# A decoder layer's ternary weights: transposes on TensorE or by DMA, and VectorE's order by the scheduler or as written

## The chip, the core and the metric

The kernel runs on one core of a Trainium2 chip. Five engines with instruction streams of their own share an SBUF of 128 partitions: PE (TensorE, matrix products and transposes into PSUM), DVE (VectorE), ACT (ScalarE), POOL (GpSimd) and SP (SyncE, which here only issues DMAs). The metric is device time in microseconds (us), lower is better.

## The reference

One layer of a decoder in float32, on x of 4 x 512 rows of 512 numbers, with a context of 4 x 1024 rows. Its three parts, cut to their core:

```python
# 1. local attention (on layernorm(x)), added to x
q = h @ wq_comp @ wq_up                       # 512 -> 128 -> 16 heads of 128
q = rmsnorm(partial_rope(q)); k = rmsnorm(partial_rope(h @ wk)); v = h @ wv
mask = (diff >= 0) & (diff < 128)             # each row sees 128 keys
probs = softmax(concat([where(mask, q k^T / sqrt(128), -1e30), sink]))
x = x + group_matmul(probs[..., :t] @ v, out_w1) @ out_w2
# 2. cross attention to the 1024 context rows, 16 heads of 32, ALiBi, masked
# 3. feed forward with quantised weights and activations
def weight_quant(w):
    scale = 1.0 / clip(mean(abs(w)), EPS)
    return clip(round(w * scale), -1.0, 1.0) / scale
# gate and up: 2048 x 512, down: 512 x 2048; einsum('bsh,oh->bso', act_quant(x), weight_quant(w))
```

The three weights of the third part are thus reduced to -1, 0 and 1 times one number for each. The products contract over the weights' last axis, so the kernel needs each of them transposed.

## The kernel before, in words

The 2048 rows are 16 tiles of 128 (`xres`, kept in SBUF). The kernel has three stages: A, local attention, up to about 690 us; B, cross attention, to about 1430 us; C, the feed forward. The diff touches stage A alone, in which the ternary weights for stage C are made beside the attention.

Stage A's unit is one tile and one group of four heads: 64 units. The main loop (L766) is a software pipeline with one unit entering in each iteration n. In this order, iteration n does: `turn` of unit n (L654: transposes of the roped queries, `qtr`); `weights` of unit n-1 (L683: exponentials on ACT, `den` and its reciprocal on DVE, the scaling of `p` on POOL); `queries` of unit n+1 (L645: the matmul `q_ps`, then `rope`); one step of `before`; `scores` of unit n (L661: `sc`, then mask, maximum and small operations on DVE); `values` of unit n-2 (L708: `av`); one step of `prep`; `turn_weights` of unit n-1 (L699: `ptr`, then `pT` on DVE). Between them `fill` (L726) takes matmuls out of generators that wait for a place:

- `before(b)` (L455) makes what batch b's units need. In each of its first four steps it normalizes a tile into `h` (L122, DVE) and transposes it (`tr_ps`, L130, PE); for batches 1 to 3 the first step also takes the statistics of four tiles (`row_stats`, L83: L88 and L89 on DVE, then `veps`, L97, and a power on POOL, L81). Two steps of `qc_ps`, four of `kv_ps` with their rope, and `ktr` follow. Batch 0 is done ahead of the loop, with statistics tile by tile; batches 1, 2 and 3 begin at iterations 0, 16 and 32, one step in each iteration.
- `fold` (L511) multiplies the two output weights into one, at the start; while it lasts (`many`) no step of `prep` is taken.
- `project` (L541) is the output projection of a finished tile, 16 matmuls `y` and one add to `xres` on DVE (L548).
- `prep` is first `ternary_weights` (L550), and from iteration 61 on `first_rows` (L741), which begins stage B: statistics of batch 0 on DVE (`norm_of`, L101), a power on POOL, `shift` and the normalized rows on ACT (L109 to L117), and their transposes.

`rope` (L435) squares on ACT, and does two products, a sum and a row sum on DVE (L442 to L448) with a power on POOL.

`ternary_weights` first reads all three weights and sums their absolute values, 12 chunks of 1 MB in 12 steps. Then it reads the 12 chunks again. A chunk is `raw`, 512 x 512 numbers in four blocks of 128 rows; six operations of DVE, three on each half (L588 to L590), turn it into the bf16 tile `tern` (one buffer). Each of two groups of eight PE transposes (L598) fills one PSUM bank, `wtr`, that ACT copies to `wst` (L603, two buffers), and SP stores that to DRAM (L606), where stage C loads it from. A chunk takes three steps; the copies are taken in the middle of the next iteration (L788).

What sets the order: inside `tc.manual_schedule(engines={PE, Activation})` (L735) the named engines keep the order in which the program emits their instructions. Instructions of the other engines, DVE among them, are put in order by a planner in the framework, which may move an instruction ahead of others that are written before it, as far as data and buffers allow. Each engine then runs its own list strictly from first to last, and waits at an instruction whose data are not there. DMAs are issued by the engine that the program names, here nearly always SP, in that engine's order.

Of the kernel before, what the change touches and what calls it, by code (L numbers as in the profile page):

```python
# [14 lines left out]
BF16 = mybir.dt.bfloat16  # L15
# [3 lines left out]
ALU = mybir.AluOpType  # L19
# [3 lines left out]
P = 128  # L23
# [17 lines left out]
MAGIC = 12582912.0  # L41
# [9 lines left out]
def decoder_layer(  # L51
# [7 lines left out]
    nc = tc.nc  # L59
# [12 lines left out]
    ident_b = const.tile([P, P], BF16, name="ident_b")  # L72
# [53 lines left out]
    def transpose_rows(pool, src, dst, tag="tr", copy=None):  # L126
# [9 lines left out]
    ternary = {  # L136
        "g": dram.tile([P, DC, FF], BF16, name="tern_g"),
        "u": dram.tile([P, DC, FF], BF16, name="tern_u"),
        "d": dram.tile([P, FC, D], BF16, name="tern_d"),
    }  # L140
# [229 lines left out]
    with tc.tile_pool(name="aw", bufs=1) as aw, tc.tile_pool(name="akv", bufs=2) as akv, \  # L370
# [7 lines left out]
        ap = early.enter_context(tc.tile_pool(name="ap", bufs=2, side="right"))  # L378
# [29 lines left out]
            out=older, in_=older, compare_op=ALU.is_ge, fill=1.0, base=0,  # L408
# [5 lines left out]
            out=older_t, in_=older_t, compare_op=ALU.is_gt, fill=0.0, base=0,  # L414
# [5 lines left out]
            out=newer_t, in_=newer_t, compare_op=ALU.is_gt, fill=1.0, base=0,  # L420
# [129 lines left out]
        def ternary_weights():  # L550

            ones = aw.tile([P, 1], F32, name="ones")
            nc.gpsimd.memset(ones, 1.0)
            invs = aw.tile([P, 3], F32, name="invs")

            def chunk(n, k):
                raw = ap.tile([P, 4, 512], F32, tag="w2", name="raw")
                w = (w_gate, w_up, w_down)[n]
                of = w[:, ts(k, 512)] if n == 2 else w[ts(k, 512)]
                nc.sync.dma_start(out=raw, in_=of.rearrange("(r p) n -> p r n", p=P))  # L560
                return raw

            for n in range(3):
                part = small.tile([P, 8], F32, tag="part", name="part", bufs=1)
                for k in range(4):
                    raw = chunk(n, k)
                    for h in range(2):
                        nc.vector.tensor_reduce(
                            part[:, 2 * k + h:2 * k + h + 1], raw[:, 2 * h:2 * h + 2, :], AX.XY, ALU.add,
                            apply_absolute_value=True,  # L570
                        )
                    yield
                tot_ps = fp.tile([P, 8], F32, tag="f", name="tot_ps")
                nc.tensor.matmul(
                    tot_ps, lhsT=ones.to_broadcast([P, P]), rhs=part, start=True, stop=True
                )
                mean = small.tile([P, 1], F32, tag="mean", name="mean", bufs=1)
                nc.vector.tensor_reduce(mean, tot_ps, AX.X, ALU.add)
                nc.vector.tensor_scalar(mean, mean, 1.0 / (FF * D), Q_EPS, ALU.mult, ALU.max)
                nc.vector.tensor_scalar(steps[:, n:n + 1], mean, 1.0 / 128.0, None, ALU.mult)  # L580
                nc.vector.reciprocal(invs[:, n:n + 1], mean)
            for n, dst in enumerate(ternary.values()):
                for k in range(4):
                    raw = chunk(n, k)
                    tern = ap.tile([P, 4, 512], BF16, name="tern", bufs=1)
                    for h in range(2):
                        r = raw[:, 2 * h:2 * h + 2, :]
                        nc.vector.tensor_scalar(r, r, invs[:, n:n + 1], -1.0, ALU.mult, ALU.max)  # L588
                        nc.vector.tensor_scalar(r, r, 1.0, MAGIC, ALU.min, ALU.add)
                        nc.vector.tensor_scalar(  # L590
                            tern[:, 2 * h:2 * h + 2, :], r, MAGIC, None, ALU.subtract
                        )
                    yield
                    for c0 in (0, 2):
                        ps = fp.tile([P, 2, 512], BF16, tag="f", name="wtr")
                        for c in range(2):
                            for r in range(4):
                                nc.tensor.transpose(  # L598
                                    ps[:, c, ts(r, P)], tern[:, r, ts(c0 + c, P)], ident_b
                                )  # L600
                        yield "copy"
                        st = ap.tile([P, 2, 512], BF16, tag="w1", name="wst")
                        nc.scalar.copy(st, ps)  # L603
                        to = dst[:, 4 * k + c0:4 * k + c0 + 2, :] if n == 2 else \
                            dst[:, c0:c0 + 2, ts(k, 512)]
                        nc.sync.dma_start(out=to, in_=st)  # L606
                        yield

        def mask_rows():

# [121 lines left out]
                        break  # L732
                    del behind[first]

        with tc.manual_schedule(engines={mybir.EngineType.PE, mybir.EngineType.Activation}):  # L735
            for i, _ in enumerate(before(0)):
                if i >= 5:
                    fill(2)
            units = [Unit(n) for n in range(NT * G)]

            def first_rows():  # L741

                rows_two = rows_of(0)
                for i in range(QT + 1):
                    next(rows_two)
                    if i % 2 == 0:
                        yield
                first.turn(0)
                yield
                first.keys(0)  # L750
                yield
                queries(0, 0)
                yield
                first.turn(1)
                yield
                queries(0, 1)
                yield
                first.keys(1)

            for b in range(1, B):  # L760
                nc.sync.dma_start(
                    out=xres[:, b * QT:(b + 1) * QT, :], in_=x[b].rearrange("(t p) d -> p t d", p=P)
                )
            units[0].queries()
            soon, prep, step = iter(()), ternary_weights(), None
            for n in range(len(units) + 2):  # L766
                if n == len(units) - 3:
                    for _ in prep:
                        pass
                    early.close()  # L770
                    bx = late.enter_context(tc.tile_pool(name="bx", bufs=1, side="right"))
                    bank.update(pool=fp, tag="f")
                    first = KeysValues(0)
                    prep = first_rows()
                if n % (QT * G) == 0 and n // (QT * G) + 1 < B:
                    soon = before(n // (QT * G) + 1)
                many = "fold" in behind
                if n < len(units):
                    units[n].turn()
                if 1 <= n <= len(units):  # L780
                    units[n - 1].weights()
                fill(2)
                if n + 1 < len(units):
                    units[n + 1].queries()
                next(soon, None)
                if n < len(units):
                    units[n].scores()
                if step == "copy":  # L788
                    step = next(prep, None)
                fill(2 if many else 1)  # L790
                if not many and n >= len(units) - 1:
                    next(prep, None)
                if n >= 2:
                    units[n - 2].values()
                fill(1 if many else 1 + n % 2)
                if not many:
                    step = next(prep, None)
                fill(1 if many else 0)
                if 1 <= n <= len(units):
                    units[n - 1].turn_weights()  # L800
                fill(1 if many else 0)
                if n == QT * G:
                    cross_weights()
                    masks = mask_rows()
                if QT * G + 10 <= n < QT * G + 15:
                    next(masks)
            for _ in prep:
                pass
            while behind:
                fill(1)  # L810
# [27 lines left out]
    with tc.tile_pool(name="b1", bufs=1) as b1, \  # L838
# [204 lines left out]
        for b in range(1, B):  # L1043
            at = KT * HG * (b - 1)
# [43 lines left out]
        with tc.manual_schedule(engines={mybir.EngineType.PE}):  # L1088
# [18 lines left out]
            for step in range(-2, KT * SETS + KT):  # L1107
                m, kt = divmod(step, KT)
                now = 0 <= step < KT * SETS
                ahead, i0 = divmod(step + 10, KT)  # L1110
# [14 lines left out]
                ps = weights(m, kt, sts) if now else None  # L1125
# [19 lines left out]
    with tc.tile_pool(name="c1", bufs=1) as c1, \  # L1145
# [6 lines left out]
                engines={mybir.EngineType.PE, mybir.EngineType.DVE, mybir.EngineType.Activation}  # L1152
# [205 lines left out]
```

## Time and profile before

| | |
|---|---|
| median of 3 runs | 1727.3 us (1725.91 to 1728.79) |
| the profiled execution | 1726.91 us, its span 1725.2 us |
| mean granted clock of TensorE | 0.987 |
| busy: PE, DVE, ACT, POOL | 1644.0, 1148.4, 946.2, 737.5 us |
| PE busy from 0 to 100 us | 81.85 us |
| PE busy from 100 to 200 us | 98.8 us |
| PE busy in each 100 us from 200 to 600 | 100 us |
| PE busy from 600 to 700 us | 96.88 us |
| `wst<-wtr`, ACT copies of the transposed ternary weights | 24 of 1.017 us, from 283.4 to 594.2 us |
| `tern<-raw`, third DVE operation of a half chunk | 24 of 0.684 us, from 255.5 to 563.7 us |

How to read it: the span is the time from the first to the last instruction of one profiled execution. A row of the timeline gives start, duration, engine, line, operation, output and inputs, shapes, and in brackets how long the engine was idle before it and what ended that. In the rows of windows, each engine has its busy time in the window and its number of instructions, then come the clock granted to TensorE (1 is full speed), the share of DMA time and GB/s. "SPq" and the like are the instruction queues that issue DMAs.

### The profile page before, as it was taken

The numbers are of one execution on the slowest core, as the hardware profiler recorded it, in microseconds if no ns is written. First come the engines' busy times: TensorE is split into PE (matmuls) and PEld (weight loads), VectorE is DVE, ScalarE is ACT, GpSimd is POOL, SyncE is SP. The second block draws the span as 40 slices with busy tenths as digits, with TensorE's granted clock in tenths as the row PEclk, the third lists the DMA queues.
The fourth block names the chain that finished last, engine by engine and source line by source line (L and its number), as shares of the span: only waits on it lengthen the run. The fifth ranks groups of instructions, "written<-read, shape, count | busy, mean of one in ns | idle before, by whom it ended". The sixth has DMA issues, their size and how long they took to land.

```text
span 1725.2 us, 23227 instructions
## 1 busy us (share of the span) xinstructions
PE 1644.0 (95%) x8064; PEld 949.4 (55%) x8096; DVE 1148.4 (67%) x2312; ACT 946.2 (55%) x1834; POOL 737.5 (43%) x470
## 2 busy tenths in 40 slices
PE   7899999999999999799999999999999978999997
PEld 4556556655655555555555555555544425666664
DVE  4555887877777662565656565656567527989996
ACT  1444455566556653145544554454566645888876
POOL 2212222322223220358878787878778970000000
PEclk9999999999999999889999999999999989999999
DMA  8421231121111000421212121211121110000000
GB/s 255 136 98 74 79 117 61 43 74 54 57 44 42 25 1 25 104 56 45 57 26 68 40 56 26 70 38 45 26 75 50 33 56 2 13 13 20 13 20 25
DMA packets 68709, 93.28 MB, mean 54 GB/s; under 512 B 23044, under 2 KB 29832, under 8 KB 68168
## 3 DMA queue, kind: packets, MB, share of 16 engines
q1 hardware_dynamic: 67296, 90.58, 17.2%
q0 software_dynamic: 1152, 1.15, 0.3%
q8 instruction: 64, 1.05, 0.2%
q14 instruction: 53, 0.43, 0.1%
q10 hardware_dynamic: 144, 0.07, 0.0%
HBM read 61.76 MB, written 10.86 MB: 42 GB/s over the span
## 4 chain that ended last, share of the span: by engine, by line
PE 81%; DVE 7%; ACT 5%; issue 3%; SPq 1%; POOL 1%; DMA 1%; ACTq 0%; POOLq 0%; DVEq 0%
PE y L544 13%; PE s_ps L870 8%; PE st L918 6%; PE sc L666 6%; PE o_ps L953 5%; PE xo_ps L1011 3%; PE q_ps L290 3%; PE q_ps L647 3%; PE av L711 3%; PE f_ps L533 3%; PE st L929 3%; PE av L713 2%; PE d_ps L1245 2%; PE y_ps L1211 2%; PE u_ps L1175 2%
## 5 line engine op out<-in xcount | busy, mean ns | idle before, releaser
L942 POOL TENSOR_TENSOR sum<-sum,p 128x1024 f32<-128x1024 f32 x190 | 446.3, 2375 | 37.8 <-ACT p L936 37.6
L874 DVE TENSOR_REDUCE nm<-s_ps 128x1 f32<-128x512 f32 x512 | 319.4, 682 | 165.4 <-PE s_ps L870 165.3
L936 ACT ACTIVATE p<-st 128x1024 f32<-128x1024 f32 x256 | 249.3, 1020 | 86.3 <-PE st L929 82.2
L544 PE MATMUL y<-wf,attnT 128*128 128x512 f32 x512 | 246.8, 592 | 0.0
L695 POOL TENSOR_TENSOR p<-p,den 128x512 f32<-128x512 f32 x64 | 67.7, 1057 | 407.9 <-ACT sq L438 252.5
L870 PE MATMUL s_ps<-ks,qs 99*128 99x512 f32 x512 | 199.9, 460 | 23.2 <-DVE nm L874 12.7
L870 PEld LDWEIGHTS s_ps<-ks,qs 99*128 99x128 f32 x512 | 88.5, 191 | 176.0 <-DVE nm L874 60.2
L918 PE MATMUL st<-qs,ks 101*128 101x512 f32 x512 | 165.9, 405 | 4.7 <-ACT p L936 4.3
L953 PE MATMUL o_ps<-p,va 128*32 128x512 f32 x1024 | 136.6, 606 | 0.0
L544 PEld LDWEIGHTS y<-wf,attnT 128*128 128x128 f32 x512 | 91.9, 190 | 73.6 <-issue 71.7
L688 ACT ACTIVATE p<-s,nm,rs 128x128 f32<-128x128 f32 x256 | 123.2, 485 | 0.9 <-DVE nm L678 0.6
L942 POOL TENSOR_TENSOR sum<-p,p 128x1024 f32<-128x1024 f32 x32 | 75.2, 2372 | 111.8 <-ACT p L936 91.6
L918 PEld LDWEIGHTS st<-qs,ks 101*128 101x128 f32 x512 | 95.6, 191 | 35.9 <-ACT p L936 20.2
L666 PE MATMUL sc<-kT,qT 128*128 128x256 f32 (+1 forms) x512 | 107.6, 353 | 0.0
L81 POOL TENSOR_TENSOR rs<-ss,neghalf 128x4 f32<-128x4 f32 (+1 forms) x72 | 82.6, 1151 | 53.4 <-DVE ss L448 52.3
L659 ACT COPY qT<-qtr 128x512 f32<-128x512 f32 x64 | 37.5, 586 | 121.5 <-PE qtr L657 121.5
L666 PEld LDWEIGHTS sc<-kT,qT 128*128 128x128 f32 x512 | 88.6, 190 | 25.8 <-issue 16.3
L720 ACT COPY attnT<-av 128x512 f32<-128x512 f32 x64 | 37.5, 587 | 86.9 <-PE av L713 70.3
L1175 PEld LDWEIGHTS <-xqT 128*128 128x128 bf16 x512 | 50.1, 98 | 48.0 <-issue 1.5
L1015 DVE TENSOR_TENSOR xres<-xo_ps,xres 128x512 f32<-128x512 f32 x64 | 44.3, 691 | 44.7 <-PE xo_ps L1011 42.4
L1011 PE MATMUL xo_ps<-wo_sb,oT 128*128 128x512 f32 x128 | 65.3, 636 | 7.6 <-POOL oT L1000 4.8
L704 DVE TENSOR_TENSOR pT<-ptr,newer_t 128x512 f32<-128x512 f32 x64 | 43.9, 686 | 40.0 <-PE ptr L702 40.0
(193 smaller groups left out, 3033.6 us busy)
## 6 DMA issues: line engine op xcount, KB each, us to landing
cx<-in_ctx SPq DMA_DIRECT2D x32, 256.0 KB
raw<-in_L_ffn_w_gate SPq DMA_DIRECT2D x8, 1024.0 KB
raw<-in_L_ffn_w_up SPq DMA_DIRECT2D x8, 1024.0 KB
raw<-in_L_ffn_w_down SPq DMA_DIRECT2D x8, 1024.0 KB
qs<-qH SPq DMA_DIRECT2D x128, 64.0 KB
w<-in_L_attn_out_w SPq DMA_DIRECT2D x4, 1024.0 KB
w<-in_L_attn_out_w SPq DMA_DIRECT2D x16, 256.0 KB
qs<-qL SPq DMA_DIRECT2D x64, 64.0 KB
```

Source lines behind the costliest of these rows:

```text
L81: nc.gpsimd.tensor_tensor(dst, src, neghalf[:, :src.shape[1]], ALU.pow)
L544: nc.tensor.matmul(y, lhsT=attnT[:, h, :], rhs=wf[:, h, :], start=(h == 0), stop=(h == HEADS - 1))
L666: nc.tensor.matmul(sc[:, h, first * P:], lhsT=self.qT[:, h, :], rhs=kT[:, (qt - 1 + first) * P:(qt + 1) * P], start=True, stop=True,)
L688: nc.scalar.activation(self.p[:, h, :], s[:, h, :], AF.Exp, bias=nm[:, h:h + 1], scale=self.rs[:, h:h + 1], accum_out=den[:, h:h + 1],)
L870: nc.tensor.matmul(s_ps, lhsT=qss[hh][0:R_TOP, g, ts(qt, P)], rhs=kss[b % 2][0:R_TOP, g, ts(hf, T)], start=True, stop=True,)
L874: nc.vector.tensor_reduce(nms[m][:, qt, g, hf:hf + 1], s_ps, AX.X, ALU.max, negate=True)
L918: nc.tensor.matmul(st[:, g % 2, :], lhsT=ks[0:R_TOP + 2, g, ts(kt, P)], rhs=qss[hh][0:R_TOP + 2, g, :], start=True, stop=False,)
L936: nc.scalar.activation(p, st, AF.Exp)
L942: nc.gpsimd.tensor_tensor(sums[m][i], last[i] if kt == 1 else sums[m][i], ps[i], ALU.add)
L953: nc.tensor.matmul(accs[m][at, :], lhsT=va[:, kt, at], rhs=ps[g // 2][:, g % 2, :], start=(kt == 0), stop=(kt == KT - 1),)
L1011: nc.tensor.matmul(y_ps, lhsT=oTs[m][:, ts(qt, P)], rhs=wo_sb[:, hh, :], start=True, stop=True)
L1175: nc.tensor.matmul(acc, lhsT=xqTs[self.t][:, c, :], rhs=w[c][:, ts(n, 512)], start=(c == 0), stop=(c == DC - 1),)
```

## The change

Three things are changed together.

First, the ternary chunks are transposed by DMA. PE's transposes, the PSUM tile `wtr` and ACT's copies are gone; in their place SP issues eight transposing DMAs for each chunk, each of which reads a 128 x 256 piece of `tern` and writes it transposed into `wst`, in SBUF. The stores to DRAM follow as before.

Second, the six DVE operations of a chunk, all in one step before, are spread over the chunk's three steps, two in each, and a chunk's load of `raw` is issued one chunk ahead, after the first operation of the chunk before it.

Third, DVE is named in the manual schedule of stage A: its instructions keep the order in which the program emits them.

```diff
-            for n, dst in enumerate(ternary.values()):
-                for k in range(4):
-                    raw = chunk(n, k)
-                    tern = ap.tile([P, 4, 512], BF16, name="tern", bufs=1)
-                    for h in range(2):
-                        r = raw[:, 2 * h:2 * h + 2, :]
+            chunks = [(n, k) for n in range(3) for k in range(4)]
+            ahead = chunk(0, 0)
+            for at, (n, k) in enumerate(chunks):
+                raw, dst = ahead, tuple(ternary.values())[n]
+                tern = ap.tile([P, 4, 512], BF16, name="tern", bufs=1)
+                halves = [raw[:, 2 * h:2 * h + 2, :] for h in range(2)]
+                for i in range(6):
+                    r, of = halves[i // 3], tern[:, 2 * (i // 3):2 * (i // 3) + 2, :]
+                    if i % 3 == 0:
                         nc.vector.tensor_scalar(r, r, invs[:, n:n + 1], -1.0, ALU.mult, ALU.max)
+                    elif i % 3 == 1:
                         nc.vector.tensor_scalar(r, r, 1.0, MAGIC, ALU.min, ALU.add)
-                        nc.vector.tensor_scalar(
-                            tern[:, 2 * h:2 * h + 2, :], r, MAGIC, None, ALU.subtract
+                    else:
+                        nc.vector.tensor_scalar(of, r, MAGIC, None, ALU.subtract)
+                    if i == 0 and at + 1 < len(chunks):
+                        ahead = chunk(*chunks[at + 1])
+                    if i % 2:
+                        yield
+                for c0 in (0, 2):
+                    st = ap.tile([P, 2, 512], BF16, tag="w1", name="wst")
+                    for r in range(4):
+                        nc.sync.dma_start_transpose(
+                            out=st[:, :, ts(r, P)], in_=tern[:, r, ts(c0 // 2, 2 * P)]
                         )
-                    yield
-                    for c0 in (0, 2):
-                        ps = fp.tile([P, 2, 512], BF16, tag="f", name="wtr")
-                        for c in range(2):
-                            for r in range(4):
-                                nc.tensor.transpose(
-                                    ps[:, c, ts(r, P)], tern[:, r, ts(c0 + c, P)], ident_b
-                                )
-                        yield "copy"
-                        st = ap.tile([P, 2, 512], BF16, tag="w1", name="wst")
-                        nc.scalar.copy(st, ps)
-                        to = ...
-                        nc.sync.dma_start(out=to, in_=st)
-                        yield
+                    to = ...
+                    nc.sync.dma_start(out=to, in_=st)
...
-        with tc.manual_schedule(engines={mybir.EngineType.PE, mybir.EngineType.Activation}):
+        with tc.manual_schedule(
+            engines={mybir.EngineType.PE, mybir.EngineType.Activation, mybir.EngineType.DVE}
+        ):
...
-                if step == "copy":
-                    step = next(prep, None)
...
-                    step = next(prep, None)
+                    next(prep, None)
```

The order of PE's other instructions, and of ACT's, is the same in both kernels. In the new order of DVE, a step of `before` stands where the loop writes it: in iteration n behind `den` and its reciprocal of unit n-1 and behind the rope of unit n+1, and ahead of mask and maximum of unit n.

More of the change, by code (lines that the diff above doesn't have):

```diff
@@ L588, in ternary_weights @@
                         nc.vector.tensor_scalar(r, r, invs[:, n:n + 1], -1.0, ALU.mult, ALU.max)
+                    elif i % 3 == 1:
                         nc.vector.tensor_scalar(r, r, 1.0, MAGIC, ALU.min, ALU.add)
-                        nc.vector.tensor_scalar(
-                            tern[:, 2 * h:2 * h + 2, :], r, MAGIC, None, ALU.subtract
-                        )
-                    yield
-                    for c0 in (0, 2):
-                        ps = fp.tile([P, 2, 512], BF16, tag="f", name="wtr")
-                        for c in range(2):
-                            for r in range(4):
-                                nc.tensor.transpose(
-                                    ps[:, c, ts(r, P)], tern[:, r, ts(c0 + c, P)], ident_b
-                                )
-                        yield "copy"
-                        st = ap.tile([P, 2, 512], BF16, tag="w1", name="wst")
-                        nc.scalar.copy(st, ps)
-                        to = dst[:, 4 * k + c0:4 * k + c0 + 2, :] if n == 2 else \
-                            dst[:, c0:c0 + 2, ts(k, 512)]
-                        nc.sync.dma_start(out=to, in_=st)
-                        yield
@@ new lines, in ternary_weights @@
+                    else:
[9 more added lines that the diff above has]
+                            out=st[:, :, ts(r, P)], in_=tern[:, r, ts(c0 // 2, 2 * P)]
+                        )
+                    to = dst[:, 4 * k + c0:4 * k + c0 + 2, :] if n == 2 else \
+                        dst[:, c0:c0 + 2, ts(k, 512)]
+                    nc.sync.dma_start(out=to, in_=st)
@@ L764, in decoder_layer @@
             units[0].queries()
-            soon, prep, step = iter(()), ternary_weights(), None
+            soon, prep = iter(()), ternary_weights()
             for n in range(len(units) + 2):
```

## The prediction

> **What bounds the kernel now.** I read the page's first two parts, then the chain of work that ended last, then the windows of the stage that the diff touches, and last the timelines of PE and DVE at the places where the order changes.
>
> ```profile
> PE 1644.0 (95%) x8064; PEld 949.4 (55%) x8096; DVE 1148.4 (67%) x2312; ACT 946.2 (55%) x1834; POOL 737.5 (43%) x470
> ...
> PE   7899999999999999799999999999999978999997
> ...
> PE 81%; DVE 7%; ACT 5%; issue 3%; SPq 1%; POOL 1%; DMA 1%; ACTq 0%; POOLq 0%; DVEq 0%
> ```
>
> TensorE is busy 95% of the span and carries 81% of the last chain. The windows say it for the part with the ternary work (columns: PE, PEld, DVE, ACT, POOL busy with instruction counts, clock, DMA share, GB/s):
>
> ```profile
> 200.00:300.00 100.00, 100.00 (x384) 58.29 (x383) 84.93 (x218) 53.04 (x156) 29.08 (x26) 1.00 0.30 107
> ...
> 500.00:600.00 100.00, 100.00 (x414) 58.22 (x413) 70.63 (x196) 60.66 (x173) 27.09 (x24) 1.00 0.09 32
> ```
>
> Between 200 and 600 us PE never waits, and DVE has 15 to 29% to spare. So PE work taken out there counts in full, ACT or DVE work taken out counts for nothing, and any new wait of PE counts in full too. PE's order is written by hand and is the same in both kernels but for the transposes taken out. What must be asked is whether DVE, until now put in order by the scheduler, still delivers in time. Two stretches of PE's timeline, the second at a group of ternary transposes:
>
> ```profile
> 224.87 1.02 PE L647 MATMUL q_ps<-wqu_sb,qcT 128*128 128x512 f32 x2
> 225.72 0.60 PE L130 MATMUL tr_ps<-ident,h 128*128 128x128 f32 x4
> 226.16 1.06 PE L666 MATMUL sc<-kT,qT 128*128 128x128 f32 x8
> ...
> 389.97 0.61 PE L598 MATMUL wtr<-ident_b,tern 128*128 128x128 bf16 x8
> 390.42 0.60 PE L702 MATMUL ptr<-ident,p 128*128 128x128 f32 x4
> ```
>
> In the first, which is iteration 16, tile 16's layernorm output h is turned straight after the next unit's query matmul, without a wait. DVE in the same microseconds, then BN and the power of 4 variances elsewhere:
>
> ```profile
> 226.03 0.16 DVE L693 TENSOR_TENSOR den<-den,es 128x4 f32<-128x4 f32 x1 [1.83 <-ACT es L692]
> 226.23 0.18 DVE L694 RECIPROCAL den<-den 128x4 f32<-128x4 f32 x1
> 226.37 0.55 DVE L122 TENSOR_SCALAR h<-xres,mv,rstd 128x512 f32<-128x512 f32 x1
> 226.83 0.42 DVE L442 TENSOR_TENSOR ra<-q_ps,cos_sb 128x256 f32<-128x256 f32 x1
> ...
> 228.15 0.42 DVE L445 TENSOR_TENSOR q<-ra,rb 128x256 f32<-128x256 f32 x1
> 228.48 0.17 DVE L448 TENSOR_SCALAR ss<-ss 128x4 f32<-128x4 f32 x1
> ...
> 599.66 0.69 DVE L88 BATCH_NORM_STATS2 stats<-xres 128x6 f32<-128x512 f32 x1
> 600.39 0.18 DVE L89 BATCH_NORM_AGGREGATE mv<-stats 128x2 f32<-128x6 f32 x1
> ...
> 35.11 1.01 POOL L81 TENSOR_TENSOR rstd<-veps,neghalf 128x4 f32<-128x4 f32 x1 [3.20 <-DVE veps L97]
> ```
>
> The h at 226.37 is that of tile 17, whose transposes come a whole iteration later: the scheduler had moved normalizations, and the statistics before them, ahead of where the program writes them. The written order has h behind the rope operations (L442 to L448).
>
> **The change part by part.** First, what goes. 24 groups of eight bf16 transposes leave PE, each 390.42 − 389.97 = 0.45 us of issue: −10.8 us, all on the path, since PE is at 100% there. 24 ACT copies of 1.017 us go too (24.4 us); ACT is busy 53 to 61%, so nothing is counted. The six ternary operations per chunk stay, spread over three slots where one slot held all; they stand before waits DVE already has (1.83 us before den in the fence), so 0. The cover is that slack; without it the two operations, 0.68 us each, would cost 1.4 us in each of 36 slots, 49 us.
>
> Second, the DMA transposes: 96 of 128x256 bf16, 64 KB each, on SP's queue, eight in a chunk, then two stores. DVE's first write to the single tern buffer of the next chunk waits for all eight. A chunk lasts three slots, 26 us (slots are 8.6 to 10.3), and from a chunk's last DVE operation to the next chunk's first write about two slots, 16 us, pass. With 7 us of DVE steps and waits between the halves, they are hidden while (26 − 7)/8 ≈ 2.4 us each holds. No transposing DMA is in this trace. Bounds from the nearest rows: from below 0.32 to 0.38 us, the issue of a ternary store by SP; from above 3.3 us, issue to landing of the 64 KB copy from SBUF to SBUF (ks from kH). The nearest in kind are 64 KB loads in 128-byte runs (wq_sb, L164): 0.65 to 1.6 us each. At 1.6 a chunk takes 8 × 1.6 + 7 ≈ 20 us: I take 0. At 3.3 it takes 33, 7 too many in 11 chunks: +77. Behind these DMAs SP has raw loads, now one chunk ahead, and mask and position loads with tens of microseconds to spare; 0 as long as the chunk fits, else they share its delay.
>
> The Trainium skill, "VectorE: DVE Perf Modes", section "The three transpose paths", speaks against the change: it gives 390 ns for a 128x128 bf16 transpose on TensorE and 1309 ns on the DMA's crossbar. The row here has a PE group of eight in 0.45 us of pitch, far less than the page's figure; no run here shows the other. By the page, as an estimate, a 128x256 costs 2.6 us, a chunk 28 us, and the sum would grow by 2 us in 11 chunks, 22 us.
>
> Third, DVE in written order. Four times for each of batches 1, 2 and 3 (iterations 0–3, 16–19, 32–35) PE's tr_ps now waits for an h that stands behind den, the reciprocal and the rope of the next unit. At iteration 16: PE is ready at 225.72. Rope's first operation can start at about 226.6 (q_ps done, h gone from ahead of it); it ends 228.65 − 226.83 = 1.8 us later, 228.4. Then h, 0.55, and PE starts at about 229.1: 3.4 us of stall. Where the residual add of a finished tile also stands ahead (iterations 17 and 33), 0.6 more: 4.0. For the first tile of a batch four pairs of statistics come between: 4 × (0.69 + 0.18, with gaps 0.9) = 3.6, veps 0.2, POOL's pow 1.0 and its handovers 0.2, so 3.4 + 5.0 = 8.4. Batch 1: 8.4 + 3 × 3.4 = 18.6; batches 2 and 3: 8.4 + 4.0 + 2 × 3.4 = 19.2 each. Sum 57.0 us. Behind the waiting h on DVE stand the mask and maximum of scores (L672, L676) of the same unit; behind tr_ps on PE stands sc of that unit, and all of PE. Bounds: 0, if something I don't see lets h start early; 12 × 8.4 = 101, if each were as long as the first.
>
> Fourth, the start. Statistics and h of tiles 0 to 3 now run tile by tile, each with a round trip to POOL, and kw_col, which waits for a load until 10.93, stands between tiles 1 and 2. Then BN (0.87), veps, pow (0.56), h (0.55) twice in a row end at about 15.9 where h ended at 12.07: +3.6 us after the transposes. Bounds 0 and 5 (two round trips).
>
> Fifth, iteration 61. Batch 0's statistics for the cross attention (L101) run late in before, from 599 on in idle time. Written, they stand after es of unit 61 (639.7): 3.6 for BN, 1.3 for the power on POOL, then ACT's shift and h (0.85 + 0.8), qT (0.6), and sc of unit 62 starts at 647 in place of 643.1: +3.9. Bounds 0 and 5.
>
> Sixth, the clock. The rows are a PE idle stretch of 3 us at 698 and what the granted clock was after, and one PE row after a shorter idle:
>
> ```profile
> 698.00:701.00 3.00, 0.05 (x1) 0.00 (x0) 0.00 (x0) 0.37 (x1) 3.00 (x7) 1.00 0.90 214
> 703.00:705.00 2.00, 1.96 (x9) 1.71 (x10) 0.03 (x1) 0.59 (x1) 0.91 (x3) 0.56 0.28 45
> 705.00:707.00 2.00, 2.00 (x6) 1.17 (x6) 1.86 (x3) 0.00 (x0) 1.21 (x3) 0.58 0.77 199
> 713.00:721.00 8.00, 6.95 (x16) 4.49 (x15) 4.56 (x9) 0.39 (x1) 0.00 (x0) 0.57 0.24 57
> ...
> 45.50 0.63 PE L657 MATMUL qtr<-ident,q 128*128 128x128 f32 x4 [2.69 <-DVE q L445]
> ```
>
> After the 3.08 us idle the clock was 0.57 for 4 us, which loses 4 × 0.43 = 1.7 us; the 8 us at 0.57 lost 3.4; after 2.69 us idle the clock stayed. The three 8.4 us stalls should bring a fall each and the nine of 3.4 to 4.0 about half of them: 7.5 × 1.7 ≈ 13 us. Bounds 0 and 12 × 3.4 = 41.
>
> The Trainium skill, "TensorE: Matmul & The Clock Gate", section "Part 1: The HAM clock gate", puts the idle that lowers the clock at a window of about 3.4 us. The 3.08 us row fell already, so it can be less. By the page alone, as an estimate, only the three long stalls are sure of a fall.
>
> Sum: 1725.2 − 10.8 + 57.0 + 3.6 + 3.9 + 13 = 1791.9 us of span. The profiled execution took 1726.91, 1.7 above its span, and the median 1727.3 is 0.4 above that: 1794.
>
> **The rivals.** A, slow transposes. If each takes over 2.4 us in turn, DVE waits at tern and with it pT and den, and PE. Each microsecond beyond is 8 × 11 = 88 us: at 3.3 about 1794 + 77 = 1871, at 4 about 1935. For it: tern has one buffer, and a transposing write lands in short pieces. Against: DMA is 9 to 30% busy in these windows.
>
> B, the other side: the normalizations don't delay PE and what is left is the PE work taken out, 1727.3 − 10.8 = 1716.5. It decides when all new waits stay below 10.8 us together, 0.9 for each of the twelve. For it: DVE is idle up to 29% there. Against: h stands behind four operations that need q_ps, and q_ps ends on PE where tr_ps begins; 1.8 + 0.55 us of DVE work can't fit in 0.9.
>
> C, the waits come, but shorter and without any fall of the clock: 12 × 3.4 = 41, the start and iteration 61 free: 1727.3 − 10.8 + 41 ≈ 1758.
>
> D, a fall at every stall: 1794 + 28 = 1822; with DMA waits of little more than a slot in all, 14 us, 1836.
>
> **How the numbers follow.** The forecast (the waits of the third part, some falls of the clock) has 0.60, C, which is its lower end, 0.10, D, its upper end, 0.13, A 0.13 and B 0.04. The range 1758 to 1836 runs from C to D and takes in the bounds of the start, of iteration 61 and of the clock; A and B lie outside, and 0.03 of C below it: 0.2 left out. A measurement here tells 0.2%, 3.5 us, from no change. Faster is B, 0.04; slower is the rest but for 0.01 in between.
>
> **What would show it.** Right: in the profile after, PE idle ended by DVE's h (L122) before tr_ps at twelve places, some 57 us, in the slices around 40–80, 225–260 and 380–410 us; the clock below 1 behind the longer ones; no wtr or wst rows and no wait of DVE at tern for a DMA; qc_ps near 18 us rather than 14.4; PE busy less by 10.8 us apart from clock. Wrong: a DVE wait before tern's third operation of many microseconds (A); tr_ps without waits (B); or stalls somewhere I haven't listed, where DVE's order lets pT or q come late in ordinary iterations. There the rows gave slack of 1 to 2 us a slot, and losing it in 64 slots would cost as much as the twelve stalls.

## The result, and the profile after

The changed kernel takes 1817.2 us (median of 4 runs, 1816.7 to 1817.5) against 1728.1 beside it: 1.0523 times as long, interval 1.051 to 1.0535, 89 us slower. Forecast were 1794 and 1758 to 1836. The profiled execution has a span of 1815.7 us (before 1725.2: +90.5) and a mean granted clock of 0.965. The page after, first the busy times, then PE and its clock in 40 slices, then the chain that ended last by engine:

```profile
PE 1666.5 (92%) x7872; PEld 957.0 (53%) x7904; DVE 1172.2 (65%) x2312; ACT 926.1 (51%) x1810; POOL 727.2 (40%) x470
...
PE   6679987998799999889999999999999987999997
...
PEclk9789998999899999888999999999999998999999
...
PE 76%; DVE 8%; ACT 7%; issue 5%; POOL 1%; SPq 1%; DMA 1%; ACTq 0%; POOLq 0%; DVEq 0%
```

PE issues 192 instructions less than before, and is busy 22.5 us longer: the clock row has notches where the PE row has them, in the slices (45 us each) of 45 to 136, 272 to 318 and 454 to 499 us. The waits of PE from 0 to 750 us (us in total, times, longest):

```profile
PE tr_ps L130 <- DVE h L122: 67.9, 15, 8.2
PE f_ps L533 <- ACT wf L538: 7.6, 10, 2.8
PE q_ps L648 <- ACT qT L660: 7.0, 1, 7.0
```

The first line has the twelve waits of batches 1 to 3 and three of the start. Before, PE had no wait for qT, and the other two lines, over the same time, were these:

```profile
PE tr_ps L130 <- DVE h L122: 9.8, 2, 9.2
PE f_ps L533 <- ACT wf L538: 3.8, 10, 0.7
```

Batch 2's four, in PE's timeline, and DVE ahead of the first and the third of them:

```profile
271.07 1.12 PE L130 MATMUL tr_ps<-ident,h 128*128 128x128 f32 x4 [8.13 <-DVE h L122]
286.06 0.66 PE L130 MATMUL tr_ps<-ident,h 128*128 128x128 f32 x4 [3.66 <-DVE h L122]
300.60 1.11 PE L130 MATMUL tr_ps<-ident,h 128*128 128x128 f32 x4 [3.58 <-DVE h L122]
313.40 0.66 PE L130 MATMUL tr_ps<-ident,h 128*128 128x128 f32 x4 [3.51 <-DVE h L122]
```

```profile
268.96 0.18 DVE L89 BATCH_NORM_AGGREGATE mv<-stats 128x2 f32<-128x6 f32 x1
269.18 0.17 DVE L97 TENSOR_SCALAR veps<-mv 128x4 f32<-128x4 f32 x1
270.47 0.55 DVE L122 TENSOR_SCALAR h<-xres,mv,rstd 128x512 f32<-128x512 f32 x1 [1.12 <-POOL rstd L81]
...
298.88 0.42 DVE L445 TENSOR_TENSOR q<-ra,rb 128x256 f32<-128x256 f32 x1
299.22 0.68 DVE L447 TENSOR_REDUCE ss<-sq 128x4 f32<-128x512 f32 x1
299.93 0.17 DVE L448 TENSOR_SCALAR ss<-ss 128x4 f32<-128x4 f32 x1
300.01 0.54 DVE L122 TENSOR_SCALAR h<-xres,mv,rstd 128x512 f32<-128x512 f32 x1
```

As forecast: statistics, power and h in the first, rope and h in the third. The clock around the first (windows: PE, PEld, DVE, ACT, POOL busy, clock, DMA share, GB/s):

```profile
262.00:267.00 5.00, 0.95 (x3) 0.12 (x1) 3.36 (x11) 1.84 (x8) 2.01 (x2) 0.94 0.57 206
267.00:271.00 4.00, 0.00 (x0) 0.00 (x0) 2.74 (x8) 0.00 (x0) 1.04 (x2) 0.50 0.00 0
271.00:276.00 5.00, 4.93 (x15) 3.63 (x16) 1.43 (x3) 1.17 (x2) 0.00 (x0) 0.50 0.00 0
276.00:280.00 4.00, 4.00 (x17) 2.34 (x16) 1.49 (x9) 0.68 (x2) 0.00 (x0) 0.92 0.00 0
```

It halves 3.5 us into the wait and stays halved for 5.6 us of work after it. The clock's loss can be summed over windows of one microsecond, as PE's busy time times what the clock lacks of 1: the first 850 us lose 41.6 us after and 9.5 before, and 25.5 of the 41.6 stand right behind the twelve waits. The DMA transposes show as this (shortest, median and longest in ns, then the first and the last start), and DVE waits for none of them at tern for more than 0.2 us:

```profile
L603 SPq DMA_TRANSPOSE wst<-tern x96: 1168/1243/1780, 340.6 to 674.5; - x96
```

### The profile page after: what moved, and what is told of

It reads as the page before. It is cut to its first block, busy times and chain, and to the rows that moved or that the text cites. A ratio compares the mean times of both kernels' runs of the same rounds, so it can differ in the third digit from the quotient of the medians.

```text
span 1815.7 us, 22979 instructions
## 1 busy us (share of the span) xinstructions
PE 1666.5 (92%) x7872; PEld 957.0 (53%) x7904; DVE 1172.2 (65%) x2312; ACT 926.1 (51%) x1810; POOL 727.2 (40%) x470
## 3 DMA queue, kind: packets, MB, share of 16 engines
q8 instruction: 63, 1.03, 0.2%
## 4 chain that ended last, share of the span: by engine, by line
PE 76%; DVE 8%; ACT 7%; issue 5%; POOL 1%; SPq 1%; DMA 1%; ACTq 0%; POOLq 0%; DVEq 0%
PE y L544 11%; PE s_ps L871 7%; PE st L919 6%; PE sc L667 6%; PE o_ps L954 5%; PE xo_ps L1012 3%; PE q_ps L290 3%; PE av L712 3%; PE f_ps L533 3%; PE st L930 3%; PE q_ps L648 3%; PE av L714 2%; PE y_ps L1212 2%; PE d_ps L1246 2%; PE tr_ps L130 2%
## 5 line engine op out<-in xcount | busy, mean ns | idle before, releaser
L544 PE MATMUL y<-wf,attnT 128*128 128x512 f32 x512 | 252.1, 603 | 0.0
L81 POOL TENSOR_TENSOR rs<-ss,neghalf 128x4 f32<-128x4 f32 (+1 forms) x72 | 73.5, 1021 | 134.2 <-DVE ss L448 133.0
L667 PE MATMUL sc<-kT,qT 128*128 128x256 f32 (+1 forms) x512 | 118.7, 382 | 0.0
L667 PEld LDWEIGHTS sc<-kT,qT 128*128 128x128 f32 x512 | 98.8, 216 | 26.7 <-issue 15.3
L130 PE MATMUL tr_ps<-ident,h 128*128 128x128 f32 x64 | 16.4, 405 | 69.0 <-DVE h L122 67.9
L533 PE MATMUL f_ps<-w,w1T 128*128 128x512 f32 x128 | 69.2, 655 | 8.0 <-ACT wf L538 7.6
L648 PE MATMUL q_ps<-wqu_sb,qcT 128*128 128x512 f32 x128 | 68.2, 615 | 7.0 <-ACT qT L660 7.0
```

The source lines that it names most:

```text
L81: nc.gpsimd.tensor_tensor(dst, src, neghalf[:, :src.shape[1]], ALU.pow)
L533: nc.tensor.matmul(f_ps, lhsT=w1T[:, c, :], rhs=w2s[n // HG][:, c, :], start=(c == 0), stop=(c == DC - 1),)
L544: nc.tensor.matmul(y, lhsT=attnT[:, h, :], rhs=wf[:, h, :], start=(h == 0), stop=(h == HEADS - 1))
L648: nc.tensor.matmul(q_ps, lhsT=made[self.b][0][:, ts(self.qt, P)], rhs=wqu_sb[:, ts(self.g, HG * P)], start=True, stop=True,)
L667: nc.tensor.matmul(sc[:, h, first * P:], lhsT=self.qT[:, h, :], rhs=kT[:, (qt - 1 + first) * P:(qt + 1) * P], start=True, stop=True,)
```

## The experiments

Beside the experiments the kernel before took 1726.1 to 1726.9 us (medians). Theory: the written order of DVE makes PE wait twelve times and the clock fall, and the DMA transposes are hidden. Rival: the DMA transposes, or the spreading of the operations, cost part of it.

**DVE alone in written order** (transposes still on PE, all six operations in one step):

```diff
-        with tc.manual_schedule(engines={PE, Activation}):
+        with tc.manual_schedule(engines={PE, Activation, DVE}):
```

> The kernel before with DVE named in the manual schedule, nothing else (transposes stay on PE). Theory: everything that the change lost and the 10.8 us of PE transposes as well: 1817 + 11 = 1828 us, with twelve waits of PE for h of 57 us in all. Rival (the DMA transposes made part of the loss): clearly under 1817 us.

Measured: 1832.4 us, 1.0613 (1.0592 to 1.0635). tr_ps waits for h 68.8 us in 15 times, q_ps at iteration 61 7.0, f_ps for wf 7.6, all as after. So this one line of the change makes the whole loss, and the other two parts give back about 15 us of it. That is 4 more than the 10.8 us of transposes; a wait that the changed kernel doesn't have is av for pT, 4.5 us in two lines, the larger one of them:

```profile
PE av L711 <- DVE pT L706: 3.4, 3, 1.7
```

**DVE left to the planner, the other two parts kept:**

```diff
-        with tc.manual_schedule(engines={PE, Activation, DVE}):
+        with tc.manual_schedule(engines={PE, Activation}):
```

> The changed kernel with DVE left to the planner again in stage A (DMA transposes and two operations per slot stay). Theory (the waits of PE for h come from the written order of DVE, and the DMA transposes are hidden): all twelve waits at tr_ps gone, the clock near that of before, and the 10.8 us of PE transposes saved: about 1728 - 11 = 1717 us. Rival (the DMA transposes or the spread operations cost time of their own, say by DVE waiting at tern): over 1728 us, up to 1800 if they made most of the loss.

Measured: 1780.2 us, 1.032 (1.03 to 1.0339). The twelve waits are gone, but 54 us are lost elsewhere, against the theory: "hidden" was not true of the DMA transposes as such. What PE waits for between 200 and 690 us, then what DVE waits for between 200 and 520, then one chunk on SP's queue and the DVE operation at tern that waits for it:

```profile
PE av L712 <- DVE pT L707: 24.4, 6, 5.9
PE ptr L703 <- ACT attnT L721: 11.2, 1, 11.2
PE sc L667 <- DVE s L673: 8.0, 3, 4.1
```

```profile
DVE tern L595 <- DMA wst<-tern: 43.2, 8, 8.4
```

```profile
316.41 10.19 SPq L603 DMA_TRANSPOSE wst<-tern  x8
...
327.83 0.69 DVE L595 TENSOR_SCALAR tern<-raw 128x1024 bf16<-128x1024 f32 x1 [4.82 <-DMA wst<-tern]
```

Eight transposes hold the queue for 10.2 us, 1.24 each. In the kernel before, the single tern buffer came free when PE had turned it, at places written by hand, and this spread the chunks from 275 to 594 us. With PE out of it, the planner runs the twelve chunks from 255 to 438 us, tern's first write mostly waiting for the transposes of the chunk before, and puts tern's write ahead of pT and the score operations, which wait with it. The clock falls at these waits too: the first 850 us lose 22.7 us, 9.5 in the kernel before.

**The same with plain copies in place of the transposes** (this kernel leaves the transposition of the weights out):

```diff
-                        nc.sync.dma_start_transpose(out=st[:, :, ts(r, P)], in_=tern[:, r, ts(c0 // 2, 2 * P)])
+                        nc.sync.dma_start(out=st[:, :, ts(r, P)],
+                            in_=tern[:, r, ts(c0 // 2, 2 * P)].rearrange("p (c q) -> p c q", c=2))
```

> The changed kernel with DVE left to the planner, and plain copies from tern to wst in place of the transposing DMAs; it leaves the transposition out, so the ternary weights in DRAM are not transposed. Same number of DMAs, same bytes, same buffers. Theory (that kernel lost its time because DVE waits at tern, 55 us in all, for eight transposes that hold the queue for 10.2 us): with copies the waits at tern mostly go and the time is 1715 to 1735 us. Rival (the planner's placing of other DVE work, or the two operations per slot, lost it): still about 1780 us.

Measured: 1729.1 us, 1.0019 (1.001 to 1.0028). The queue's time for one copy, and DVE's waits at tern between 150 and 720 us:

```profile
L603 SPq DMA_DIRECT2D wst<-tern x96: 593/621/986, 255.6 to 393.0; - x96
```

```profile
DVE tern L595 <- DMA wst<-tern: 8.4, 7, 3.2
```

Half the time on the queue, a fifth of the wait, and 51 of the 54 us are back. The theory on that kernel, that the queue's time for the transposes is what DVE waits for, stands. The 10.8 us of PE are not seen as a gain even here: PE still waits 11.5 us between 200 and 690 us, where the kernel before didn't.

**The clock.** Idle matmuls, whose result is never read, in front of the twelve transposes keep PE at work while it waits:

```diff
                 normalize(h, b * QT + i, i % at_once, mv, rstd)
+                if b:
+                    idle = fp.tile([P, T], F32, tag="f", name="idle")
+                    for _ in range(8 if i else 18):
+                        nc.tensor.matmul(idle, lhsT=ident, rhs=made[b - 1][0], start=True, stop=True)
```

> The changed kernel with idle matmuls of 128x512, never read, in front of the twelve tr_ps of batches 1 to 3: 18 for a batch's first tile, 8 for the others, 0.43 us each, so that PE works while it waits. They add work that changes no result. Theory (the falls of the clock after the waits are a cost of their own; summed over the rows of one microsecond after the twelve waits, PE's busy time times what is missing of the clock, they are 25.5 us): the waits turn into work of the same length, the clock stays at 1 there, 1817 - 25 = 1792 us. Rival (the slow clock costs nothing because PE would wait anyway): 1817 us or a little more.

Measured: 1842.3 us, 1.0675 (1.0656 to 1.0694). The size was wrong: such a matmul is two records, 0.86 us and not 0.43, so the idle work was 3 x 15.5 + 9 x 6.9 = 108 us where the waits had been 57. The loss of clock did drop, from 41.6 to 13.4 us (counted up to 870 us here, since the same work comes later). With half of them (9 and 4):

> As the run with idle matmuls before, but the matmuls fitted to the waits: one 128x512 float32 matmul takes two records of 0.43 us, 0.86 us, so 9 (7.7 us) ahead of a batch's first tile and 4 (3.4 us) ahead of the others. No result changes. Theory (a fall of the clock after each of the twelve waits costs 25.5 us in all, beside the waits): 1817 - 25 = 1792 us, the clock at 1 around the twelve places. Rival (the slow clock hides behind other waits): 1817 us.

Measured: 1796.4 us, 1.0405 (1.039 to 1.0419), 20 us less than the changed kernel by the ratios. One of batch 2's places, where PE now works up to h:

```profile
270.33 3.60 PE L467 MATMUL idle<-qcT,ident 128*128 128x512 f32 x8
274.15 0.66 PE L130 MATMUL tr_ps<-ident,h 128*128 128x128 f32 x4 [0.23 <-DVE h L122]
```

The lost clock is 15.3 us, 26.3 less than after, of which about 20 show in the time. A kernel that does more work, of no use, is faster: the fall of the clock is a cost beside the wait.

**h and its statistics written earlier**, DVE still in written order: a generator writes a batch's statistics at the ends of the four iterations before, and each h at the end of the iteration before its transposes (for batch 1, ahead of the loop).

```diff
+        def rows_ahead(b):
+            ...                       # bn_stats, bn_aggr: one tile, yield; veps, power: yield
+            for i in range(QT):
+                h = ap.tile([P, D], F32, name="h", bufs=1)
+                normalize(h, b * QT + i, i, mv, rstd)
+                rows_made[b, i] = h
+                yield
...
-                normalize(h, b * QT + i, i % at_once, mv, rstd)
+                h = rows_made.pop((b, i))
...
                 fill(1 if many else 0)
+                next(ahead_of, None)
+                if n % (QT * G) == QT * G - 1 - (QT + 1) and n // (QT * G) + 2 < B:
+                    ahead_of = rows_ahead(n // (QT * G) + 2)
```

> The changed kernel, DVE still in written order, with statistics of batches 1 to 3 written over the four or five iterations before they are used, and each h written at the end of the iteration before its transposes. PE's order stays. Theory: the twelve waits (57.1 us) and their falls of the clock (25.5 us) go: 1817 - 83 = 1734 us; what stays over 1717 is the start, iteration 61 (7.0 us wait and 3.1 us of clock) and some waits for wf. Rival (DVE in written order makes other work late as soon as h is out of the way, or the DMA transposes do): 1745 us or more.

Measured: 1742.1 us, 1.0093 (1.0078 to 1.0109), 8 more than expected. PE's waits from 60 to 690 us:

```profile
PE f_ps L556 <- ACT wf L561: 7.6, 8, 2.8
PE q_ps L671 <- ACT qT L683: 7.0, 1, 7.0
PE tr_ps L130 <- DVE h L122: 3.9, 5, 1.1
```

The twelve waits have shrunk to some 4 us, and 75 of 89 us are gone: the place of h and its statistics in DVE's order was the cause. What is left over the time before is the wait at iteration 61, those for wf, and the start.

**How far the transposes are hidden.** On that kernel each DMA transpose is issued two and three times, into the same place (`for r in range(8)`, or 12, with `r % 4`):

> The kernel with rows written ahead (1742 us), each DMA transpose issued three times, the last two repeating the first into the same place: 24 for a chunk. Theory (prediction: hidden up to about 2.4 us each, each microsecond beyond costs 88 us; one takes 1.24 us by the profile, three 3.7 us): DVE now waits at tern in eleven chunks, + 60 to + 115 us, 1800 to 1857 us. Rival (a transposing DMA blocks only its queue, the chunk has far more room): 1742 us.

> The kernel with rows written ahead (1742 us), each DMA transpose issued twice: 2.49 us for each piece, just at the bound of the prediction of 2.4. Tripled, DVE waited 97 us at tern in eleven chunks, 8.8 each, and a single step from two to three is 8 x 1.24 = 9.9 us per chunk. Theory: nearly hidden, 0 to 15 us: 1742 to 1757 us. Rival (each repetition costs the same): half of the tripled loss, 1742 + 44 = 1786 us.

Measured: three times 1829.7 us, 1.0598 (1.0583 to 1.0612), twice 1744.0, 1.0097 (1.0081 to 1.0112), once 1742.1. With three, DVE waits eleven times:

```profile
DVE tern L618 <- DMA wst<-tern: 97.0, 11, 12.4
```

With two, it waits twice, 1.9 and 2.8 us in the last two chunks, and PE's own waits between 250 and 690 us grow by no more than 0.3 us:

```profile
DVE tern L618 <- DMA wst<-tern: 4.8, 2, 2.8
```

The threshold is thus real: at 1.24 us nothing is paid, at 2.49 us two of the twelve chunks reach it, and PE doesn't feel it yet. Three times cost 88 us, 8.0 a chunk; the queue needs 24 x 1.243 = 29.8 us for a chunk, so 21.8 fit on the mean, 2.7 us for each of eight.

**A kernel with the remaining waits taken away as well:**

```diff
-                mv, rstd = layernorm_stats(b * QT + i, 1)
+                ...                   # statistics of tile i+1 ahead of h of tile i (batch 0)
...
-                transpose_rows(fp, w1, w1T, tag="y", copy=nc.vector.tensor_copy)
+                transpose_rows(fp, w1, w1T, tag="f", copy=nc.vector.tensor_copy)
...
             units[0].queries()
+            fill(3)
...
+                if n == len(units) - 14:
+                    ahead_of = norm_ahead(0, QT)
```

> The kernel with rows written ahead, and four more moves: statistics of tile i+1 written ahead of h of tile i at the start, kw_col and nsink behind the four first tiles; batch 0's statistics for the cross attention written at iterations 51 to 54 in place of 61; the turned out_w1 in PSUM banks of the other tag, so that f_ps never shares a bank with them; three matmuls of the fold ahead of the first turn. Theory: it takes away the 7.0 us wait of iteration 61 and its fall of the clock (1.5), 4 us of waits for wf and their falls (3.3), about 2.5 us at the start, 2.4 us before the first qtr with its fall (1.7): 1742 - 22 = 1720 us. Rival (something else binds in DVE's written order): 1735 us or more.

Measured: 1716.3 us, 0.9939 (0.9925 to 0.9952). It is faster than both kernels. Whether that is owed to the change was asked by putting its parts back into this kernel, and the other way round by putting two of the moves (the banks of the turned out_w1, `fill(3)`) into the kernel before.

> The tuned kernel (1716 us) with the ternary chunks as before the change: six DVE operations in one step, transposes on PE and copies on ACT; DVE in written order. Theory: 10.8 us of PE come back, and, as in the kernel with DVE written and PE transposes, about 4.5 us of waits of av for a pT that stands behind the six operations, with a fall or two of the clock (1.7 each): 1716 + 11 + 5 + 2 = 1734 us. Rival (the gain over before is the other moves, the transposes were nearly free on PE): 1716 to 1721 us.

> The tuned kernel with a chunk's six DVE operations in one step again, the DMA transposes in the next step and a third step without work, so a chunk still takes three. Theory: the spreading alone is worth the waits of av for pT, about 4.5 us and their falls: 1716 + 4.5 to 8 = 1721 to 1724 us. Rival (six operations fit the slack as well): 1716 us.

> The kernel before with the two moves of the tuned kernel that concern PE's order and banks at the start (turned out_w1 in the banks of the other tag, three matmuls of the fold ahead of the first turn); DVE by the planner, transposes on PE. Theory: they take away 2.7 us before the first qtr and up to 3.8 us of waits for wf: 1727 - 3 to 6 = 1721 to 1724 us, so that about half of the tuned kernel's gain is theirs. Rival (these waits only move): 1727 us.

Measured: PE transposes and one step 1733.3 us, 1.0036 (1.0022 to 1.005); DMA transposes and one step 1728.5, 1.0011 (0.9999 to 1.0022); the kernel before with the two moves 1714.8, 0.9935 (0.992 to 0.9949). PE's waits in the second of them, the one that shows the spreading, from 200 to 640 us, and in the third from 0 to 200:

```profile
PE tr_ps L149 <- DVE h L141: 5.7, 4, 3.4
PE av L755 <- DVE pT L750: 5.4, 3, 2.4
PE av L755 <- DVE pT L748: 1.2, 1, 1.2
```

```profile
PE tr_ps L130 <- DVE h L122: 9.6, 2, 8.8
PE ktr L500 <- POOL kn L493: 0.9, 1, 0.9
PE qc_ps L468 <- ACT hT L131: 0.7, 1, 0.7
```

With h and DVE's order in hand, the DMA transposes and the spreading together are worth 0.0097 of 1727, 17 us; the spreading has 12 of it, where 5 to 8 were expected: 5.0 us of waits for pT (6.6 against 1.6 in the tuned kernel), 2.2 of waits for h (5.7 against 3.5) and 4.6 of lost clock (18.8 against 14.2). But the kernel before with two moves of PE's order, DVE left to the planner and the transposes on PE, is as fast as the tuned one within the intervals. It gained 12 us where 3 to 6 were expected: the waits for wf, w1T and the first qtr that are gone make about 8 of them, the rest isn't assigned. So written order, even with h and the statistics moved by hand, costs as much as DMA transposes and spreading bring: with PE transposes in both, 1733 stands against 1715. DMA transposes in the planner's order at a pace of their own were not tried.

## Why the prediction was right, and where its sum was off

By terms of the span, forecast and measured:

| term | forecast | measured |
|---|---|---|
| PE transposes | -10.8 | -10.8 (the row; no run has it alone) |
| twelve waits for h | 57.0 | 57.1 |
| start | 3.6 | 2.1 more of waits at tr_ps |
| iteration 61 | 3.9 | 7.0 |
| clock, first 850 us | 13 | 32.1 (41.6 against 9.5) |
| waits for wf | 0 | 3.8 (7.6 against 3.8) |
| sum | 66.7 | 91.3; the span grew by 90.5 |

The table leaves out what is smaller, such as 1.6 us less of waits for w1T. PE's busy time fits it: 22.5 us more are 10.8 less for the transposes and 33.3 more, nearly all of it the slower clock's.

- **The twelve waits** came out in sum and singly: 8.18, 8.13 and 8.13 for 8.4; 3.5 to 3.7 for 3.4; with the residual add 4.30 for 4.0 at iteration 33. At iteration 17 it was 3.66 for 4.0; the add that was forecast there stands at iteration 18. That the sum agrees to 0.1 us is luck: the three long waits came out 0.8 shorter together and the others 0.9 longer. That written order is their cause is shown: left to the planner or moved by hand, they go.
- **The clock** is the term that was mis-sized. "The nine of 3.4 to 4.0 about half of them" was too few: all twelve waits brought a fall, and a fall cost 2.1 us on the mean and not 1.7 (25.5/12). Three further waits brought falls too (1.7 and 1.7 us behind a qtr and an f_ps, 3.1 behind iteration 61). The row of 3.08 us, from which a fall was priced, has a second wait of 1.21 us behind it, with 0.70 us of work between, and the clock fell only after that one. That the clock is a cost of its own is shown by the idle matmuls.
- **Iteration 61** waited 7.0 for 3.9. The sum counted four statistics operations of L88, each with its L89, ahead of the power; DVE's timeline has eight there, and all sixteen, those of the other batches too, from 722 to 784 us. The prediction misread the trace before: there the sixteen stand singly, the first four, batch 0's, at 178, 215, 263 and 275 us with their power at 276, and the four from 599 us on are the last batch's. The planner had thus taken batch 0's much earlier than the prediction says. That written order puts them into iteration 61 and that PE waits for them was right.
- **wf** was not foreseen. In the kernel before, the sums of the fold (f_ps) and the turned out_w1 changed places in two PSUM banks, so that f_ps waited sometimes for DVE and sometimes for ACT; in the changed kernel it waits nearly always for ACT, and in the two longest waits, 2.77 and 1.91 us, the wf copy stands behind four exponentials. That the planner hands out the buffers in its own order too is what the instructions' waits say; that it made the 3.8 us is argued and not shown. The tuned kernel, with the banks apart, has no wait for wf.
- **The start** was a little less than forecast; qc_ps began at 16.99 us, 2.6 later than before, where the text had 18.
- **DMA transposes at 0** held for the changed kernel, and the bound was close: 2.4 forecast, 2.7 on the mean by the tripled run, with two chunks waiting at 2.49. (The wq_sb loads named as nearest in kind took 0.54 to 1.75 us, not 0.65 to 1.6, which changes nothing.) What the working did not see is that this cover is the work of the change's own third part: DVE in written order starts the chunks' transposes 22 to 40 us apart (twelve chunks from 340 to 676 us). Without it (1780 us) rival A takes place at 1.24 us each. Spreading the six operations, which the sum took at 0, saves 12 us in the tuned kernel.
- Of the rivals, B and C are excluded by the waits and the clock; D, a fall at every stall, is what happened. That its 1822 lies only 5 us from the time is in part luck: it priced the falls at 41 us where 32 were lost, and lacked 7 us of waits at iteration 61 and for wf.

On the two rules of the Trainium skill: by "VectorE: DVE Perf Modes", section "The three transpose paths", 22 us would have been added, as an estimate, for 2.6 us per piece; the queue shows 1.24 us for twice the page's 128x128, and no cost. By "TensorE: Matmul & The Clock Gate", section "Part 1: The HAM clock gate", with a window of about 3.4 us, three falls were sure by the prediction's estimate; here each of the twelve waits, from 3.51 us up, brought one, and so did two shorter ones, of 2.40 and 1.91 us. The grid of 3.41 us on which the clock changes here (last section) agrees with the window's length.

## What to carry to other kernels

When an engine's list is switched from a planner to written order, look in the trace for its instructions that stood ahead of their place; each of them becomes a wait of the engine that they feed, and the length of the wait can be read off: the durations of what now stands in front. Ask of every single-buffered tile what paced it; taking the consumer off a hand-ordered engine also takes the pacing away. Where the matrix engine has no slack, add to each wait of 3.5 us or more some 2 us for the clock, as measured here.

## What was not expected of the hardware

- Whether a short wait lowers the clock isn't decided by its length alone: of waits of PE before, 2.69 us brought no fall; after, 2.40 us at the same place brought one (1.7 us), 2.77 none, and 1.91 one. What decides it can be read from the clock records of the traces: the clock is either 1 or 0.5, and in every run all its changes lie on a grid of 3.41 us. In the changed kernel each fall from 20 to 760 us comes at the end of a step of this grid in which PE was busy 44% of the time or less, and no step at full clock that was under 57% went without one; in other runs a few steps of 42 to 48% did. The waits of 2.40 and 1.91 us left 30% and 44% of one step busy; that of 2.77 us lay across two steps with 59% and 60%, that of 2.69 us before across two with 51% and 63%. A fall in the changed kernel lasts one to three whole steps, and a step full of work loses half of 3.41, 1.7 us.
- Useless matmuls paid: 54 us of them in place of 57 us of waits saved 20 us.
- A transposing DMA of 64 KB takes 1.24 us of its queue, a plain copy of the same 64 KB between the same tiles 0.62; eight of the first kept the queue busy for 10.2 us.
